# A four-layer graph network kernel: row products issued a stripe later, left terms spread earlier, and layer 2 in a fixed order

## The chip, the cores and the metric

The kernel runs on one core of one Trainium2 chip. The metric is the device time of one execution in microseconds (us), the median of several runs. In the text PE is TensorE (matrix products), DVE is VectorE, ACT is ScalarE, POOL is GpSimd, and SP is the queue that starts the large loads. SBUF is the working memory, and PSUM the memory into which PE writes[...].

## What is computed

x is 4096x64 and adj is a 4096x4096 matrix of zeros and ones, both float32. Four layers follow one another, each of the form x = layernorm(x + layer(x)). adj is read anew from main memory in each, 64 MiB a time. The reference, cut to what matters here:

```python
# layer 0: mean over the neighbours
h_neigh = (adj @ X + X) / deg;  out = relu(concat([X, h_neigh]) @ W + b);  out / norm(out)

# layers 1 and 3: attention in hyperbolic space, over all pairs (i, j)
left, right = x_t @ w_att[:D, 0], x_t @ w_att[D:, 0]
adj_att = sigmoid(left[:, None] + right[None, :] + b_att) * adj
x_local = logmap(x[:, None, :], x[None, :, :], c)
support_t = einsum('ij,ijd->id', adj_att, x_local);  proj(expmap(x, support_t, c), c)

# layer 2: weights that halve with the rank of a neighbour, counted from the end of the row
support = input @ weight                       # the "row products"
rank = cumsum(mask, axis=1);  k = min(deg, 100);  pos = rank - (deg - k)
w = mask * where(pos > 0, 0.5 ** (k - pos), 0);   out = w @ support + bias
```

## The kernel before

The 4096 receiving rows are cut into 4 **stripes** of 1024 (`GROUPS` = 3, 2, 1, 0), the sending rows into 32 **blocks** j of 128, taken from 31 down to 0. One **unit** is one stripe by one block: a tile of 128 x 1024 pairs. Each layer has 4 x 32 = 128 units. One load brings two blocks of one stripe (1 MiB).

The work on rows between the layers (normalisation, the curved step `move`, the row products `linear`, the preparation `prepare` of the next layer) is written as generators. They are queued with `later`, and `tick` takes a few steps of the queue after each unit, first come first served:

```python
def tick(n):
    while n and waiting:
        if next(waiting[0][1], False) is False: waiting.pop(0)
        else: n -= 1

def rsqrt(a, name):                              # 1/sqrt by bits and three Newton steps, on [P, 8]
    half = row.tile([P, n], I32, name="rs_half")
    V.tensor_scalar(half, a.bitcast(I32), 1, None, ALU.logical_shift_right)
    V.tensor_scalar(r.bitcast(I32), half, -1.0, float(0x5F3759DF), ALU.mult, ALU.add)
    for _ in range(3): ...                       # tensor_mul and two scalar_tensor_tensor each
```

Layers 1 and 3. `attend` is one stripe; DVE has two passes over each 128x1024 tile, ACT two, PE six products into `zp` and two (in float32, each issued as two) into `acc`:

```python
def attend(layer, s, left_b, sb, ps, rate):
    acc = ps.tile([P, W], F32, name="acc")
    for g in reversed(range(NB // 2)):
        _, edge = load(s, g)
        need((layer, 2 * g // WB))               # takes queue steps until this group's rows are there
        for k in (1, 0):
            zp = ps.tile([P, WW], F32, name="zp")            # two banks, 2 such tiles
            ...                                              # L861, L864, L867: products into zp
            nc.scalar.activation(sig, left_b, AF.Sigmoid, bias=right[:, j : j + 1])       # L869
            nc.scalar.activation(sq, zp, AF.Square, bias=turn, scale=-1.0 / UNIT)         # L873
            V.scalar_tensor_tensor(t, zp, 0.0, sig, ALU.max, ALU.mult)                    # L875
            V.scalar_tensor_tensor(t, sq, HIGH**2, t, ALU.add, ALU.mult)                  # L876
            ...                                              # L878: acc += xe[j] x t
            tick(rate)
    sums = sb.tile([P, W], F32, name="sums", bufs=1)
    nc.scalar.copy(sums, acc)                                # L884
    return sums

def attention(layer, x, x_new, curve, rates, behind):        # behind: linear (layer 1), store (layer 3)
    with ExitStack() as lp:                                  # pools of its own for each layer
        sb, ps = ...                                         # SBUF bufs=2; PSUM bufs=2
        need((layer, GROUPS[0])); left_b = spread_left(GROUPS[0])
        for n, s in enumerate(GROUPS):
            sums = attend(layer, s, left_b, sb, ps, rates[n])
            if n + 1 < NW: left_b = spread_left(GROUPS[n + 1])
            later((layer + 1, s), move(s, x, x_new, sums, curve, layer == 1), behind(s, x_new))
```

`spread_left` (8 transposes on PE, L837, two ACT copies, L842) puts the stripe's left terms on all partitions; every sigmoid of the stripe reads it. `move` turns a stripe's sums into its new rows: some 16 queue steps with three `rsqrt`, mostly a chain of DVE operations on [128, 8], from the transposes L891 to the sum x_new at L992. `linear` is 4 steps: transposes of the new rows (L1001), ACT copy (L1004), products with the weights (L1008), ACT (L1016) and DVE (L1017) into `halves`, which layer 2 multiplies by. `spread_left`, `move` and `linear` all take their PSUM tiles from `aux`, which has 2 buffers.

Layer 2 takes two stripes in turns. z holds running counts of neighbours in PSUM, w = 2^-z:

```python
with ExitStack() as lp:                          # pools of its own: d2_own, d2_sb (3), d2_ps (2)
    ...                                          # enter, pass_by: 0/1 matrices made here
    for n in range(0, NW, 2):
        two = GROUPS[n : n + 2]
        zs, accs = ..., ...                      # a z of two banks and an acc of one for each
        for g in reversed(range(NB // 2)):
            ...                                  # load and, for odd g, check(s, g, a) on DVE (L692)
            for k in (1, 0):
                for i, edge in enumerate(edges):
                    ...                          # L1209: 4 products into z (2 pass_by, 2 enter)
                    nc.scalar.activation(w, z, AF.Exp, bias=at_edge, scale=-LN2)          # L1217
                    ...                          # L1220: 4 products of w and halves[j] into acc
                    tick(1)
        for s, acc in zip(two, accs):
            nc.scalar.copy(sums, acc)            # L1230
            later((3, s), end_2(s, sums), prepare(s, x_3, ...))
```

The order of the instructions on each engine is otherwise not that of the text: the framework that compiles the kernel sorts them by a model of its own, within what data and buffers allow.

Of the kernel before, what the change touches and what calls it, by code (L numbers as in the profile page):

```python
# [10 lines left out]
F32 = mybir.dt.float32  # L11
# [10 lines left out]
D = 64  # L22
# [36 lines left out]
def gnn_stack_kernel(  # L59
# [511 lines left out]
    def stream(fits):  # L571

        with ExitStack() as st:
# [3 lines left out]

            keep = pool("f_keep")
            xs = pool("f_xs", 3)
            loads = pool("f_loads", 5)  # L580
            row = pool("f_row")
            lefts = pool("f_lefts", 2)
            aux = pool("f_aux", 2, space=PSUM)
# [44 lines left out]
            def rsqrt(a, name):  # L628

                n = a.shape[1]  # L630
                half = row.tile([P, n], I32, name="rs_half")
                V.tensor_scalar(half, a.bitcast(I32), 1, None, ALU.logical_shift_right)
                r, t = nums(name, n), nums("rs_t", n)
                V.tensor_scalar(
                    r.bitcast(I32), half, -1.0, float(0x5F3759DF), ALU.mult, ALU.add
                )
                for _ in range(3):
                    V.tensor_mul(t, r, r)
                    V.scalar_tensor_tensor(t, t, -0.5, a, ALU.mult, ALU.mult)
                    V.scalar_tensor_tensor(r, t, 1.5, r, ALU.add, ALU.mult)  # L640
                return r
# [200 lines left out]
                    nc.scalar.copy(to[:, h * W : (h + 1) * W], t)  # L842
                return to

            def attend(layer, s, left_b, sb, ps, rate):


                acc = ps.tile([P, W], F32, name="acc")
                for g in reversed(range(NB // 2)):
                    _, edge = load(s, g)  # L850
                    need((layer, 2 * g // WB))
                    for k in (1, 0):
                        j = 2 * g + k
                        of = slice(j * P, (j + 1) * P)

                        zp = ps.tile([P, WW], F32, name="zp")
                        for h in range(2):
                            half = zp[:, h * W : (h + 1) * W]
                            to = slice(s * WW + h * W, s * WW + (h + 1) * W)
                            at = k * WW + h * W  # L860
                            nc.tensor.matmul(  # L861
                                half, two_i, edge[:, at : at + W], start=True, stop=False
                            )
                            nc.tensor.matmul(  # L864
                                half, hi_lo[:, of], lo_hi[:, to], start=False, stop=False
                            )
                            nc.tensor.matmul(half, src[:, of], dst[:, to], start=False, stop=True)  # L867
                        sig = sb.tile([P, WW], F32, name="sig")
                        nc.scalar.activation(  # L869
                            sig, left_b, AF.Sigmoid, bias=right[:, j : j + 1]  # L870
                        )
                        sq = sb.tile([P, WW], F32, name="sq")
                        nc.scalar.activation(sq, zp, AF.Square, bias=turn, scale=-1.0 / UNIT)  # L873
                        t = sb.tile([P, WW], F32, name="t", bufs=3)
                        V.scalar_tensor_tensor(t, zp, 0.0, sig, ALU.max, ALU.mult)  # L875
                        V.scalar_tensor_tensor(t, sq, HIGH**2, t, ALU.add, ALU.mult)  # L876
                        for h in range(2):
                            nc.tensor.matmul(  # L878
                                acc[h * D : (h + 1) * D, :], xe[:, j, :], t[:, h * W : (h + 1) * W],
                                start=j == BLOCKS[0], stop=j == BLOCKS[-1],  # L880
                            )
                        tick(rate)
                sums = sb.tile([P, W], F32, name="sums", bufs=1)
                nc.scalar.copy(sums, acc)  # L884
                return sums

            def to_rows_of(sums):

# [130 lines left out]
                )  # L1019


            x0 = xs.tile([P, NB, D], F32, name="x")
            for s in GROUPS:
                nc.sync.dma_start(x0[:, blocks(s), :], x_in[:, blocks(s), :])
            x1 = xs.tile([P, NB, D], F32, name="x")
            with ExitStack() as lp:
# [47 lines left out]
                for s in GROUPS:  # L1074
# [49 lines left out]
                        prepare(s, x1, att1, batt1_sb, curve1, 1e-15, good[:, 0]),  # L1124
                    )

            def attention(layer, x, x_new, curve, rates, behind):
                with ExitStack() as lp:
                    sb = lp.enter_context(tc.tile_pool(name="n_sb", bufs=2))
                    ps = lp.enter_context(tc.tile_pool(name="n_ps", bufs=2, space=PSUM))  # L1130
                    need((layer, GROUPS[0]))
                    left_b = spread_left(GROUPS[0])
                    for n, s in enumerate(GROUPS):
                        sums = attend(layer, s, left_b, sb, ps, rates[n])
                        if n + 1 < NW:
                            left_b = spread_left(GROUPS[n + 1])
                        later(
                            (layer + 1, s), move(s, x, x_new, sums, curve, layer == 1),
                            behind(s, x_new),
                        )  # L1140


            x_2 = xs.tile([P, NB, D], F32, name="x")
# [3 lines left out]


            x_3 = xs.tile([P, NB, D], F32, name="x")
            with ExitStack() as lp:  # L1150
                own = lp.enter_context(tc.tile_pool(name="d2_own", bufs=1))
                sb = lp.enter_context(tc.tile_pool(name="d2_sb", bufs=3))
                ps = lp.enter_context(tc.tile_pool(name="d2_ps", bufs=2, space=PSUM))


                enter = own.tile([P, P], BF16, name="enter")
                pass_by = own.tile([P, P], BF16, name="pass_by")
                edge_of = own.tile([P, P], BF16, name="edge_of")
                V.tensor_scalar(edge_of, ident, OFF_EDGE, None, ALU.mult)
                V.memset(pass_by, 1.0)  # L1160
                nc.gpsimd.affine_select(
                    out=enter, in_=pass_by, compare_op=ALU.is_gt, fill=0.0, base=0,
                    pattern=[[-1, P]], channel_multiplier=1,
                )
                V.tensor_sub(enter, enter, edge_of)
                V.tensor_sub(pass_by, pass_by, enter)
                at_edge = num(own, "at_edge", 1)
                V.memset(at_edge, -(OFF_EDGE + CUT) * LN2)

                def end_2(s, sums):  # L1170
                    z = grp("z0")
                    t = to_rows_of(sums)
                    yield 1
                    V.scalar_tensor_tensor(
                        z.rearrange("p (h k) f -> p h k f", h=2)[:, 0], t[:, 0], 2.0**CUT / SUP,
                        b2_sb[:, None, :].to_broadcast([P, SB, D]), ALU.mult, ALU.add,
                    )
                    V.scalar_tensor_tensor(
                        z.rearrange("p (h k) f -> p h k f", h=2)[:, 1], t[:, 1], 2.0**CUT / SUP,
                        b2_sb[:, None, :].to_broadcast([P, SB, D]), ALU.mult, ALU.add,  # L1180
                    )
                    yield 1
                    V.tensor_add(z, z, x_2[:, blocks(s), :])
                    yield 1
                    yield from norm_rows(x_3, s, z, x2[:, blocks(s)])

                for n in range(0, NW, 2):
                    two = GROUPS[n : n + 2]
                    zs = [ps.tile([P, WW], F32, name="z") for _ in two]

                    accs = [ps.tile([P, W], F32, name="acc") for _ in two]
                    behind = [None, None]
                    for g in reversed(range(NB // 2)):
                        edges = []
# [6 lines left out]
                        for k in (1, 0):  # L1201
                            j = 2 * g + k
                            for i, edge in enumerate(edges):
                                z, acc = zs[i], accs[i]
                                here = edge[:, k * WW : (k + 1) * WW]
                                for lhs, rhs in ((pass_by, behind[i]), (enter, here)):
                                    for h in range(0, WW, W):
                                        if rhs is not None:
# [3 lines left out]
                                                skip_group_check=True,  # L1212
                                            )
                                behind[i] = here

                                w = sb.tile([P, WW], BF16, name="w")
                                nc.scalar.activation(w, z, AF.Exp, bias=at_edge, scale=-LN2)  # L1217
                                for part in range(2):
                                    for h in range(2):
                                        nc.tensor.matmul(  # L1220
                                            acc[h * D : (h + 1) * D, :],
                                            halves[:, j, part * D : (part + 1) * D],
                                            w[:, h * W : (h + 1) * W],
                                            start=j == BLOCKS[0] and part == 0,
                                            stop=j == BLOCKS[-1] and part == 1,
                                        )
                                tick(1)
                    for s, acc in zip(two, accs):
                        sums = row.tile([P, W], F32, name="sums2", bufs=2)
                        nc.scalar.copy(sums, acc)  # L1230
                        later(
                            (3, s), end_2(s, sums),
                            prepare(s, x_3, att3, batt3_sb, curve3, 1e-30, good[:, 1]),
# [96 lines left out]
```

## Time and profile before

| | |
|---|---|
| time, median of 3 runs | 1259.73 us (1249.18 to 1260.44) |
| the profiled execution | 1248.49 us, span 1246.8 us |
| busy PE, DVE, ACT | 1064.1, 981.3, 811.4 us of the span |
| layer 0 | 0 to about 216 us |
| layer 1, its four stripes' sums (L884) | 313, 396, 497, 604 us |
| layer 2, first and second pair of stripes | 619.5 to 734, and to 857 us |
| layer 3, then the last rows | 857 to 1219, and to 1246.8 us |

The stages are read from the first and last start of each line's instructions, and the copies of the sums. A table of stages gives, for each stretch, the us in which each engine was busy with the number of instructions in brackets, then the granted clock of PE as a share of full speed, the share of the DMA engines, and GB/s. A timeline row gives start, duration, engine, line, operation, count, and in square brackets how long the engine was idle before and which instruction released it. The busy time of PE counts overlapping products once, but the end of a product is modelled, so the distance between starts tells more than durations do.

### The profile page before, as it was taken

How to read it: one execution, taken by the hardware profiler on the slowest of the kernel's cores; microseconds unless marked ns; L12 is line 12 of the kernel's file. 1: busy time of each engine (PE TensorE's matmuls, PEld its weight loads, DVE VectorE, ACT ScalarE, POOL GpSimd, SP SyncE). 2: the span in 40 equal slices, each digit the busy share in tenths (PEclk: the TensorE clock that was granted, in tenths of full speed). 3: DMA queues.
4: the chain of work that ended last, by engine and by line, in shares of the span. 5: the costliest groups of instructions: out<-in, count | busy, mean ns of one | idle time of the engine just before them, and what ended most of it. 6: DMA issues, size and time to landing. Idle time of an engine off the chain costs nothing.

```text
span 1246.8 us, 13844 instructions
## 1 busy us (share of the span) xinstructions
PE 1064.1 (85%) x4818; PEld 393.4 (32%) x4907; DVE 981.3 (79%) x2081; ACT 811.4 (65%) x833; POOL 49.6 (4%) x85
## 2 busy tenths in 40 slices
PE   5879788899998899798598898898889999899990
PEld 2345445232222322322232223332333333222220
DVE  5486876999997799599663347535999999999996
ACT  0021213889886787587365668767889888788870
POOL 0010101000000000000100000000000000001001
PEclk9989899899999799699699999999999999999996
DMA  7989898555554366155177887688345555565510
GB/s 280 400 338 335 313 357 324 186 175 203 202 203 169 109 201 229 68 203 186 51 268 271 295 313 265 241 295 299 134 152 201 203 202 203 182 204 204 203 34 20
DMA packets 40144, 271.83 MB, mean 218 GB/s; under 512 B 6016, under 2 KB 6272, under 8 KB 7296
## 3 DMA queue, kind: packets, MB, share of 16 engines
q1 hardware_dynamic: 37440, 269.50, 61.0%
q10 hardware_dynamic: 2624, 1.35, 0.4%
q8 instruction: 40, 0.66, 0.2%
q14 instruction: 40, 0.33, 0.1%
HBM read 269.78 MB, written 1.05 MB: 217 GB/s over the span
## 4 chain that ended last, share of the span: by engine, by line
DVE 40%; PE 40%; ACT 12%; DMA 4%; issue 3%; POOL 1%; another core or an unknown queue 0%; ACTq 0%; POOLq 0%; SPq 0%; DVEq 0%
DVE t L875 14%; DVE t L876 13%; PE acc L878 7%; PE z L1209 6%; PE acc L1220 6%; ACT w L1217 5%; PE zp L861 4%; PE zp L864 4%; PE zp L867 4%; PE acc L1087 4%; ACT sq L873 3%; DVE junk L692 3%; DMA edges<-in_adj_dram 2%; PE aux L1008 2%; PE aux L775 1%
## 5 line engine op out<-in xcount | busy, mean ns | idle before, releaser
L873 ACT ACTIVATE sq<-zp,turn 128x1024 f32<-128x1024 f32 x256 | 285.1, 1114 | 84.1 <-PE zp L867 52.9
L875 DVE SCALAR_TENSOR_TENSOR t<-zp,sig 128x1024 f32<-128x1024 f32 x256 | 311.3, 1219 | 15.3 <-ACT sq L873 12.9
L876 DVE SCALAR_TENSOR_TENSOR t<-sq,t 128x1024 f32<-128x1024 f32 x256 | 311.0, 1220 | 0.8
L869 ACT ACTIVATE sig<-left_b,right 128x1024 f32<-128x1024 f32 x256 | 292.1, 1143 | 19.9 <-DVE t L875 18.0
L878 PE MATMUL acc<-t,xe 128*64 128x512 f32 x1024 | 282.2, 624 | 16.6 <-DVE t L876 15.9
L692 DVE SCALAR_TENSOR_TENSOR junk<-edges 128x2048 bf16<-128x2048 f32 x64 | 146.4, 2288 | 94.2 <-DMA edges<-in_adj_dram 94.2
L861 PE MATMUL zp<-edges,two_i 128*128 128x512 bf16 x461 | 181.3, 393 | 37.8 <-DVE t L875 34.1
L864 PE MATMUL zp<-lo_hi,hi_lo 128*128 128x512 f16 x512 | 195.5, 382 | 3.7 <-issue 0.4
L867 PE MATMUL zp<-dst,src 74*128 74x512 f16 x512 | 196.7, 384 | 0.0
L1217 ACT ACTIVATE w<-z,at_edge 128x1024 bf16<-128x1024 f32 x128 | 136.1, 1113 | 76.3 <-PE z L1209 74.0
L861 PEld LDWEIGHTS <-two_i 128*128 128x128 bf16 x512 | 50.2, 98 | 178.9 <-issue 141.7
L1220 PE MATMUL acc<-w,halves 128*64 128x512 bf16 x512 | 80.9, 393 | 25.0 <-ACT w L1217 24.5
L1087 PE MATMUL acc<-edges,first 128*128 128x512 bf16 x240 | 79.0, 406 | 16.7 <-DMA edges<-in_adj_dram 16.3
L878 PEld LDWEIGHTS acc<-t,xe 128*64 128x64 f32 x1024 | 51.8, 136 | 124.5 <-DVE t L876 64.6
L1209 PE MATMUL z<-edges,enter 128*128 128x512 bf16 x245 | 85.4, 393 | 2.2 <-DVE k L909 1.6
L1087 PE MATMUL acc<-edges,third 128*65 128x512 bf16 x256 | 83.2, 407 | 0.8 <-issue 0.2
L867 PEld LDWEIGHTS <-src 74*128 74x128 f16 x512 | 49.4, 96 | 101.0 <-issue 42.2
L864 PEld LDWEIGHTS <-hi_lo 128*128 128x128 f16 x512 | 50.1, 98 | 86.0 <-issue 50.3
L1209 PE MATMUL z<-edges,pass_by 128*128 128x512 bf16 x237 | 75.0, 394 | 1.7 <-issue 1.5
L1220 PEld LDWEIGHTS <-halves 128*64 128x64 f16 x512 | 24.1, 108 | 75.6 <-issue 74.6
L1107 ACT COPY top<-acc 128x512 f32<-128x512 f32 x8 | 4.7, 588 | 63.7 <-PE acc L1087 63.7
L1209 PEld LDWEIGHTS <-enter 128*128 128x128 bf16 x256 | 24.2, 97 | 52.3 <-issue 28.9
(255 smaller groups left out, 784.4 us busy)
## 6 DMA issues: line engine op xcount, KB each, us to landing
edges<-in_adj_dram SPq DMA_DIRECT2D x256, 1024.0 KB, 5.0
x<-in_x_dram SPq DMA_DIRECT2D x4, 256.0 KB, 3.9
out_dram<-x ACTq DMA_DIRECT2D x4, 256.0 KB, 2.5
att_sb<-in_L_gnn_w_att_dram ACTq DMA_DIRECT2D x1, 64.0 KB, 7.3
att_sb<-in_L_gnn_att_w_dram ACTq DMA_DIRECT2D x1, 64.0 KB, 6.1
w_sb<-in_L_gnn_W_dram ACTq DMA_DIRECT2D x1, 32.0 KB, 3.7
b_sb<-in_L_gnn_b_dram ACTq DMA_DIRECT2D x1, 32.0 KB, 4.1
b_sb<-in_L_gnn_bias_dram ACTq DMA_DIRECT2D x1, 32.0 KB, 5.2
```

The lines of the kernel that those rows point to most:

```text
L692: V.scalar_tensor_tensor(junk, a, 0.0, a, ALU.not_equal, ALU.not_equal, accum_out=odd[:, n : n + 1])
L861: nc.tensor.matmul(half, two_i, edge[:, at : at + W], start=True, stop=False)
L864: nc.tensor.matmul(half, hi_lo[:, of], lo_hi[:, to], start=False, stop=False)
L867: nc.tensor.matmul(half, src[:, of], dst[:, to], start=False, stop=True)
L869: nc.scalar.activation(sig, left_b, AF.Sigmoid, bias=right[:, j : j + 1])
L873: nc.scalar.activation(sq, zp, AF.Square, bias=turn, scale=-1.0 / UNIT)
L875: V.scalar_tensor_tensor(t, zp, 0.0, sig, ALU.max, ALU.mult)
L876: V.scalar_tensor_tensor(t, sq, HIGH**2, t, ALU.add, ALU.mult)
L878: nc.tensor.matmul(acc[h * D : (h + 1) * D, :], xe[:, j, :], t[:, h * W : (h + 1) * W], start=j == BLOCKS[0], stop=j == BLOCKS[-1],)
L1087: nc.tensor.matmul(accs[h][:m], lhs[:, j, :], edge[:, at : at + W], start=j == BLOCKS[0], stop=j == BLOCKS[-1],)
L1209: nc.tensor.matmul(z[:, h : h + W], lhs, rhs[:, h : h + W], start=j == BLOCKS[0], stop=True, skip_group_check=True,)
L1217: nc.scalar.activation(w, z, AF.Exp, bias=at_edge, scale=-LN2)
```

## The change

It does five things. (1) Row products: `behind` (in layer 1, `linear`) is no longer queued with its stripe's `move`, but after the next stripe's `attend`, ahead of that stripe's `move`. (2) Left terms: `spread_left` for the next stripe is issued at the load g = 2 of the running one, six units ahead of its end. (3) Layer 2 has a fixed order on PE and ACT, that of the text; in it, the products L1220 of a unit are put off (`lag`) until after the next unit's products into z. (4) Pools: attention and layer 2 share one SBUF and one PSUM pool, opened once; w takes the place of `sq`; the 0/1 matrices are made at the start of the kernel; and the loads have 6 buffers in place of 5. (5) `rsqrt` makes its first guess with one DVE operation in place of two.

The diff, cut to its core (left out are the moved lines that make the 0/1 matrices, and `end_2`, which is moved unchanged):

```diff
-            loads = pool("f_loads", 5)
+            loads = pool("f_loads", 6)
@@ rsqrt
-                half = row.tile([P, n], I32, name="rs_half")
-                V.tensor_scalar(half, a.bitcast(I32), 1, None, ALU.logical_shift_right)
                 V.tensor_scalar(
-                    r.bitcast(I32), half, -1.0, float(0x5F3759DF), ALU.mult, ALU.add
+                    r.bitcast(I32), a.bitcast(I32), -0.5, float(0x5F3759DF), ALU.mult, ALU.add
                 )
@@ attend
-            def attend(layer, s, left_b, sb, ps, rate):
+            def attend(layer, s, left_b, rate, then):
+                next_left = None
                     need((layer, 2 * g // WB))
+                    if g == 2 and then is not None:
+                        next_left = spread_left(then)
-                        zp = ps.tile([P, WW], F32, name="zp")
+                        zp = ps.tile([P, WW], F32, name="z")
-                sums = sb.tile([P, W], F32, name="sums", bufs=1)
+                sums = row.tile([P, W], F32, name="sums", bufs=2)
-                return sums
+                return sums, next_left
@@ attention
+            sb = pool("p_sb", 2)
+            ps = pool("p_ps", 2, space=PSUM)
             def attention(layer, x, x_new, curve, rates, behind):
-                    for n, s in enumerate(GROUPS):
-                        sums = attend(layer, s, left_b, sb, ps, rates[n])
-                        if n + 1 < NW:
-                            left_b = spread_left(GROUPS[n + 1])
-                        later(
-                            (layer + 1, s), move(s, x, x_new, sums, curve, layer == 1),
-                            behind(s, x_new),
-                        )
+                behind_of = None
+                for n, s in enumerate(GROUPS):
+                    then = GROUPS[n + 1] if n + 1 < NW else None
+                    sums, left_b = attend(layer, s, left_b, rates[n], then)
+                    if behind_of is not None:
+                        later((layer + 1, behind_of), behind(behind_of, x_new))
+                    later((layer + 1, s, "x"), move(s, x, x_new, sums, curve, layer == 1))
+                    behind_of = s
+                later((layer + 1, behind_of), behind(behind_of, x_new))
@@ layer 2
+            lag = []
+            def flush():
+                while lag:
+                    lag.pop(0)()
+            with tc.manual_schedule(engines={mybir.EngineType.PE, mybir.EngineType.Activation}):
                 for n in range(0, NW, 2):
...
                                 behind[i] = here
+                                flush()
-                                w = sb.tile([P, WW], BF16, name="w")
+                                w = sb.tile([P, WW], F32, name="sq").bitcast(BF16)[:, :WW]
                                 nc.scalar.activation(w, z, AF.Exp, bias=at_edge, scale=-LN2)
-                                for part in range(2):
-                                    for h in range(2):
-                                        nc.tensor.matmul(acc[...], halves[...], w[...], ...)
+                                def add(acc=acc, j=j, w=w):
+                                    ...          # the same four products
+                                lag.append(add)
                                 tick(1)
+                    flush()
```

## The prediction

> **What bounds the kernel now.** I read the table of stages first, because the share of busy time of the whole span (PE 85%, DVE 79%) mixes stages with different limits. I cut the span where a line starts or ends: at the copies of the stripes' sums and at the first work after them.
>
> ```profile
> core 0: us, PE busy (x) PEld busy (x) DVE busy (x) ACT busy (x) POOL busy (x), PEclk, DMA share, GB/s
> 313.00:396.00 83.00, 80.10 (x322) 24.46 (x324) 81.70 (x140) 69.89 (x67) 1.28 (x1) 1.00 0.60 204
> 396.00:413.00 17.00, 8.63 (x38) 6.80 (x37) 5.99 (x17) 6.98 (x12) 2.21 (x2) 0.64 0.14 56
> 413.00:497.00 84.00, 81.08 (x314) 24.53 (x319) 80.78 (x141) 68.10 (x64) 0.63 (x1) 0.97 0.57 192
> 497.00:514.00 17.00, 8.95 (x38) 6.97 (x37) 5.62 (x14) 7.05 (x12) 2.38 (x2) 0.58 0.10 41
> 514.00:602.00 88.00, 78.21 (x298) 23.47 (x303) 84.11 (x141) 66.44 (x61) 0.46 (x1) 0.96 0.52 179
> 602.00:619.50 17.50, 9.81 (x34) 6.06 (x36) 7.98 (x25) 4.39 (x8) 2.05 (x3) 0.50 0.00 1
> 619.50:734.00 114.50, 102.51 (x516) 33.89 (x524) 48.79 (x115) 69.69 (x70) 2.63 (x2) 0.99 0.77 272
> 734.00:857.00 123.00, 107.97 (x603) 38.47 (x613) 60.27 (x173) 90.55 (x97) 4.26 (x14) 0.99 0.79 280
> ```
>
> Within a stripe of layer 1 (313 to 396, 413 to 497) DVE is busy 81.7 of 83 and 80.8 of 84 us: DVE is the bound there. The groups say why:
>
> ```profile
> L875 DVE SCALAR_TENSOR_TENSOR t<-zp,sig 128x1024 f32<-128x1024 f32 x256 | 311.3, 1219 | 15.3 <-ACT sq L873 12.9
> L876 DVE SCALAR_TENSOR_TENSOR t<-sq,t 128x1024 f32<-128x1024 f32 x256 | 311.0, 1220 | 0.8
> ```
>
> Two passes of 1.22 us for 128 units are 312 us a layer; nothing in the change touches them. Layer 3 has the same loop, so layers 1 and 3 can lose only idle DVE time, and that lies between stripes: from 396 to 413 and from 497 to 514 DVE works 6.0 and 5.6 of 17 us, and from 602 to 619.5 it works 8.0. The boundaries of layer 3 show no such hole. The chain of waits names what fills the first one:
>
> ```profile
> 397.75 1.57 POOL w_att L988
> ...
> 405.06 1.97 PE aux L1008 x8
> 407.03 2.05 PE aux L837 x8
> ```
>
> `move` of the stripe before ends (L988, L992), then its row products run one engine after another (L1001, L1004, L1008 from 400.1 to 407.0), and only then the left terms of the next stripe (L837), without which no sigmoid can start; the next z on PE (L861) comes at 413.4. So 17 us are a queue for the two `aux` buffers: the left terms depend on none of this and merely come later in the text. Why does a `move` whose first transpose (L891) is at 314 end only at 399? The timeline of DVE:
>
> ```profile
> 389.63 0.22 DVE L973 TENSOR_SCALAR n<-n,k_rsc 128x8 f32<-128x8 f32 x1
> 389.76 1.22 DVE L876 SCALAR_TENSOR_TENSOR t<-sq,t 128x1024 f32<-128x1024 f32 x1
> ...
> 390.90 0.16 DVE L974 TENSOR_SCALAR n<-n 128x8 f32<-128x8 f32 x1
> 390.97 1.22 DVE L876 SCALAR_TENSOR_TENSOR t<-sq,t 128x1024 f32<-128x1024 f32 x1
> ```
>
> Its chain of short operations gets one turn between two long passes: some 65 dependent steps of 1.25 us are a whole stripe of 82 us.
>
> Layer 2 is another regime. ACT and PE, in turns, there:
>
> ```profile
> 672.08 2.12 ACT L1217 ACTIVATE w<-z,at_edge 128x1024 bf16<-128x1024 f32 x2 [1.43 <-PE z L1209]
> 675.63 2.12 ACT L1217 ACTIVATE w<-z,at_edge 128x1024 bf16<-128x1024 f32 x2 [1.43 <-PE z L1209]
> ```
>
> ```profile
> 673.24 0.62 PE L1220 MATMUL acc<-w,halves 128*64 128x512 bf16 x4 [0.36 <-ACT w L1217]
> 673.80 0.62 PE L1209 MATMUL z<-edges,pass_by 128*128 128x512 bf16 x2
> ```
>
> A pair of units takes 3.55 us (672.08 to 675.63). ACT does two exps in 2.12 us and then waits 1.43 us for z. PE waits too, 0.36 us for w, at the head of each such cycle. Neither is full: both exps run together, and PE then has products for both. The largest work is PE's. From starts, two products 0.22 to 0.23 us apart (a row of two lasts 0.61, a single one 0.39), so 4 into z are 0.90 us; the 4 into acc, which lie in two halves of the array, 0.56 us (673.24 to 673.80). A unit is 1.46 us of PE against 1.06 of ACT.
>
> **What the Trainium skill says.** "PSUM — Partial Sum Buffer", section "Engine vs sequencer instructions": products start and complete in the order of the program, and the queues of ScalarE and VectorE are strict first in, first out. The trace agrees: L837 sits behind L1008 although its data are older. It also means that a fixed order holds every exp behind whatever row work stands in front of it. "Perfetto Trace Analysis", section "Optimization Strategy": with several regimes one treats each by itself and looks for what blocks in the gaps of its engine; a gap that repeats can mean that there are too few buffers. Layer 2 has such a gap, but here the order on PE makes it, for both z exist. "TensorE: Matmul & The Clock Gate", section "HAM oscillation — how this bites in real kernels": PE that idles falls to half its clock. The table agrees, 0.64, 0.58 and 0.50 in the three gaps; so the first products after a gap are slow as well.
>
> **The change part by part.**
>
> *Row products and left terms, layer 1.* Both 17 us gaps should close, as `linear` now follows a `move` that had a whole stripe, and the left terms are there before the stripe ends. The 11.6 us of DVE work in the gaps do not vanish: they go into stripes where DVE is full. I allow 1.5 us a boundary for the sums and refilling, as in layer 3 (DVE idle of 1.3 to 2.8 us a stripe by the table). Gain: 34 − 11.6 − 3 = **19 us**.
>
> *Into layer 2.* The third `move` now starts later, behind a `linear`, so it isn't done when layer 1 ends. When its stripe is over, the remaining steps have DVE to themselves, 0.2 us each. In the fixed order PE's first row work in layer 2 is the `linear` of that stripe; it holds PE until x_new is there. I estimate 8 us of the 17.5 remain (15 to 20 steps at 0.2 us, POOL's 1.57, DVE's 0.69, the first exp's table). Layer 2 has idle DVE time, so the rest is gained: **9 us**. The shared pools are needed for this, as nothing waits for a pool to be given back.
>
> *Layer 2.* In the new order, PE does z(u+1) between z(u) and the acc products of u. From the end of z(u), 0.1 us to the exp (the last product ends at 675.53, the exp starts at 675.63), 1.11 of exp, 0.05 to PE (673.19 to 673.24) are 1.26 us; PE has acc(u−1) and z(u+1) to do meanwhile, 1.46 us. So PE needn't wait: a pair is 2.92 us, and 64 pairs take 187 against 227 us. DMA: a pair needs 1 MiB, 361 GB/s; layer 0 reached 409 in a stretch of 25 us (50 to 75), and the sixth buffer gives room. On PE then comes the row work that was hidden in the slack: two `linear` (3.4 us each: twice 0.6 and 1.1, from layer 0's rows), two `prepare` (four sets of transposes at 0.91, and 0.34), sums to rows, together 18 us. Last, stalls of the fixed order: a Square, a cast, a tanh or a transpose stands in the queue when DVE has yet to compute its input, perhaps behind a 2.28 us `check`. Some five such places for each of two prepared stripes and three for the `move`, each 0.5 to 2 us: 12 us by estimate. The sum is 217 us against 237.5: **20 us**.
>
> *Small ones.* One operation less in each `rsqrt`: about 28 of them lie in DVE-bound stretches, 0.1 us each in between long passes, and three in the last rows: **3 us**. Left terms ahead of time in layer 3: **3 us**. The sixth buffer in layer 0, where DMA moves 334 GB/s over the layer but 409 in its best stretch: the short stops at the stripes' ends may close a little, **3 us**.
>
> Together 57 us.
>
> **The rivals.** *(a) The fixed order eats its own gain.* ACT in layer 2 has 0.40 us of slack a unit; the copies of `prepare` take 1.01 each, and only one unit is held back in `lag`. Against it: the text leaves whole steps between a DVE operation and its reader in several places, and only some 80 of 128 units have a step. If stalls were 30 us instead of 12, layer 2 would gain nothing, and the kernel would be at 1215. *(b) A gap moves instead of closing.* `move` plus a late `linear` may spill over each stripe, some 10 us more each time, and be paid before layer 2: PE would stand 15 us or more. For it: a `move` fills its stripe already. The time would be about 1206. *(c) DMA becomes the bound in layer 2.* At 2.92 us a pair the tiles held by `behind` and `check` leave few loads in flight; at layer 0's mean of 334 GB/s a pair takes 3.14 us, and 14 us of the gain go. *(d) All better:* with stalls near nothing, and the table's full 17.5 us gained, 1175.
>
> **Range and chances.** The profiled span is 1246.8, the median 12 above it, the lowest run 2. From the middle of the measured times, 1254, less 57: 1196 us, with its uncertainty mostly in layer 2 (0 to 35 us) and at its entry (0 to 15). Range 1168 to 1224. Faster by over 2% means below 1234.5, which needs only half of layer 1's and a part of layer 2's gain: 0.91. Within 2%: 0.07. Slower: 0.02, if the order of the whole program shifts for the worse.
>
> **What would show it.** In the profile after: stripes of layer 1 end some 84 us apart with no stretch where DVE is under 8 tenths, and L837 before each L884; first exp within 10 us of the last L884 of layer 1; ACT's waits for z (74 us by the waits of now) falling to a third, exps 1.46 us apart in the stretches without row work, and PE's clock at full there; layer 2's first exp to last L1230 near 217 us. The prediction is wrong if exps stay 1.7 us apart or more because PE waits for loads or ACT stands behind row work, or if DVE in layer 1 idles at other places.

## The result, and the profile after

| | before | after |
|---|---|---|
| time, median | 1255.7 us (4 runs) | 1209.26 us (4 runs, 1208.16 to 1209.93) |
| ratio, 95% interval | | 0.9633 (0.9579 to 0.9687) |
| span of the profiled execution | 1246.8 us | 1206.4 us |

The prediction was 1196 us, range 1168 to 1224. The chain of stages, cut at the copies of the stripes' sums (L884 and L1230 before, L886 and L1248 after), shows where the 40.3 us of span came from:

| stage | before | after | difference |
|---|---|---|---|
| layer 0 and first stripe of layer 1 | 313.8 | 311.7 | −2.1 |
| second stripe | 82.5 | 82.3 | −0.1 |
| third stripe | 100.9 | 89.6 | −11.3 |
| fourth stripe | 107.0 | 95.7 | −11.3 |
| layer 2, from the sums of layer 1 to its own last sums | 252.5 | 234.9 | −17.6 |
| layer 3 | 362.0 | 364.1 | +2.1 |
| last rows | 28.2 | 28.1 | 0.0 |

Differences are taken before rounding. The medians differ by 46.4 us: the profiled execution of before took 7 us less than its median, that of after 1 us less, so 6 us of the gain are in no stage of this table.

The table of stages of the changed kernel, in the columns of the one shown for before:

```profile
394.00:411.00 17.00, 15.23 (x59) 4.68 (x59) 16.30 (x25) 13.72 (x14) 1.97 (x1) 1.00 0.60 218
...
484.00:500.00 16.00, 15.74 (x65) 4.90 (x63) 15.68 (x28) 14.32 (x14) 0.00 (x0) 1.00 0.60 219
...
579.50:590.40 10.90, 1.99 (x8) 1.01 (x10) 7.25 (x28) 1.00 (x3) 1.21 (x1) 0.50 0.00 1
590.40:697.00 106.60, 103.98 (x550) 33.72 (x550) 46.58 (x114) 74.49 (x74) 2.84 (x2) 0.99 0.81 290
697.00:814.50 117.50, 109.06 (x610) 35.40 (x610) 61.20 (x169) 88.77 (x93) 9.34 (x14) 0.97 0.80 291
```

Where the first hole of layer 1 was, DVE is busy 16.3 of 17 us, and 15.7 of 16 where the second was. A hole is left ahead of layer 2 (579.5 to 590.4), with PE at half clock. The exps in layer 2, by groups: they wait for z 52 us instead of 74, where I had forecast a third of 74.

```profile
L1228 ACT ACTIVATE sq<-z,at_edge 128x1024 bf16<-128x1024 f32 x128 | 142.1, 1113 | 52.6 <-PE z L1219 52.3
```

The timeline of an undisturbed stretch, ACT and then PE. Each row is one exp, or the products of half a unit:

```profile
641.15 1.11 ACT L1228 ACTIVATE sq<-z,at_edge 128x1024 bf16<-128x1024 f32 x1 [0.45 <-PE z L1219]
642.71 1.11 ACT L1228 ACTIVATE sq<-z,at_edge 128x1024 bf16<-128x1024 f32 x1 [0.45 <-PE z L1219]
```

```profile
642.54 0.62 PE L1235 MATMUL acc<-sq,halves 128*64 128x512 bf16 x4
643.09 0.62 PE L1219 MATMUL z<-edges,pass_by 128*128 128x512 bf16 x2
643.56 0.61 PE L1219 MATMUL z<-edges,enter 128*128 128x512 bf16 x2
644.10 0.62 PE L1235 MATMUL acc<-sq,halves 128*64 128x512 bf16 x4
644.65 0.62 PE L1219 MATMUL z<-edges,pass_by 128*128 128x512 bf16 x2
```

The exps are 1.56 us apart, against 1.78 (half of a pair of 3.55) before, and PE has no bracket, so it doesn't wait. But 1.56 is not the 1.46 of the prediction. From start to start, the two pass_by products take 0.47 us, the two enter products ahead of acc 0.54, and the four acc products 0.55. Two products inside z take 0.45 elsewhere (see x8).

The entry of layer 2, PE:

```profile
588.41 1.03 PE L1003 MATMUL aux<-ident,x 128*64 128x128 f32 x4 [9.13 <-DVE x L994]
```

The fixed order has the transposes of the third stripe's new rows here (L1003), and they wait for the last step of that stripe's `move` (L994).

### The profile page after: what moved, and what is told of

Same layout as the page of the kernel before. It is cut to its first block, busy times and chain, and to the rows that moved or that the text cites. A ratio compares the mean times of both kernels' runs of the same rounds, so it can differ in the third digit from the quotient of the medians.

```text
span 1206.4 us, 13877 instructions
## 1 busy us (share of the span) xinstructions
PE 1063.5 (88%) x4907; PEld 381.6 (32%) x4907; DVE 975.7 (81%) x2035; ACT 812.8 (67%) x831; POOL 56.2 (5%) x85
## 4 chain that ended last, share of the span: by engine, by line
PE 46%; DVE 40%; ACT 6%; DMA 4%; issue 3%; POOL 1%; ACTq 0%; POOLq 0%; DVEq 0%; SPq 0%
DVE t L877 13%; DVE t L878 11%; PE acc L880 9%; PE z L1219 8%; PE z L863 6%; PE z L869 5%; PE z L866 5%; PE acc L1235 4%; PE acc L1106 4%; DVE junk L690 4%; ACT sq L875 3%; DMA edges<-in_adj_dram 2%; PE aux L773 2%; PE aux L1010 1%; ACT sq L1228 1%
## 5 line engine op out<-in xcount | busy, mean ns | idle before, releaser
L875 ACT ACTIVATE sq<-z,turn 128x1024 f32<-128x1024 f32 x256 | 285.0, 1113 | 78.7 <-PE z L869 52.8
L877 DVE SCALAR_TENSOR_TENSOR t<-z,sig 128x1024 f32<-128x1024 f32 x256 | 311.4, 1219 | 15.0 <-ACT sq L875 11.9
L880 PE MATMUL acc<-t,xe 128*64 128x512 f32 x1024 | 289.1, 625 | 15.9 <-DVE t L878 15.6
L863 PE MATMUL z<-edges,two_i 128*128 128x512 bf16 x512 | 201.6, 394 | 28.2 <-DVE t L877 24.1
L869 PE MATMUL z<-dst,src 74*128 74x512 f16 x512 | 196.5, 384 | 0.0
L866 PE MATMUL z<-lo_hi,hi_lo 128*128 128x512 f16 x512 | 195.3, 381 | 0.0
L1228 ACT ACTIVATE sq<-z,at_edge 128x1024 bf16<-128x1024 f32 x128 | 142.1, 1113 | 52.6 <-PE z L1219 52.3
L1106 PE MATMUL acc<-edges,first 128*128 128x512 bf16 x256 | 82.5, 402 | 17.5 <-DMA edges<-in_adj_dram 17.2
L1235 PE MATMUL acc<-sq,halves 128*64 128x512 bf16 x512 | 81.2, 397 | 9.1 <-ACT sq L1228 9.1
L869 PEld LDWEIGHTS <-src 74*128 74x128 f16 x512 | 49.4, 96 | 98.5 <-issue 40.3
L1219 PE MATMUL z<-edges,enter 128*128 128x512 bf16 x256 | 79.9, 394 | 0.0
L773 PE MATMUL aux<-ident,ys 128*128 128x128 f16 (+1 forms) x192 | 19.1, 268 | 28.7 <-DVE ys L754 28.7
```

What stands on the lines that cost most here:

```text
L863: nc.tensor.matmul(half, two_i, edge[:, at : at + W], start=True, stop=False)
L866: nc.tensor.matmul(half, hi_lo[:, of], lo_hi[:, to], start=False, stop=False)
L880: nc.tensor.matmul(acc[h * D : (h + 1) * D, :], xe[:, j, :], t[:, h * W : (h + 1) * W], start=j == BLOCKS[0], stop=j == BLOCKS[-1],)
L1106: nc.tensor.matmul(accs[h][:m], lhs[:, j, :], edge[:, at : at + W], start=j == BLOCKS[0], stop=j == BLOCKS[-1],)
L1219: nc.tensor.matmul(z[:, h : h + W], lhs, rhs[:, h : h + W], start=j == BLOCKS[0], stop=True, skip_group_check=True,)
```

## The experiments

In each set the kernel before ran on the same chip, and its median moves by up to 8 us from set to set; so ratios are compared first. A profile gives the lengths of stages.

| run | median us | ratio to before (95%) |
|---|---|---|
| the change | 1209.3 | 0.9633 (0.9579 to 0.9687) |
| x1 parts (1) and (2) alone | 1230.9 | 0.985 (0.9803 to 0.9897) |
| x3 no fixed order | 1204.6 | 0.9644 (0.9588 to 0.97) |
| x4 no late acc products | 1386.4 | 1.109 (1.1014 to 1.1166) |
| x5 row products at once | 1232.3 | 0.9876 (0.9848 to 0.9903) |
| x6 left terms at the end | 1207.8 | 0.9669 (0.9646 to 0.9692) |
| x7 empty steps ahead of row products | 1191.1 | 0.9543 (0.9519 to 0.9566) |
| x8 acc products in pairs | 1199.8 | 0.9602 (0.9578 to 0.9626) |
| x9 five load buffers | 1215.8 | 0.9732 (0.9685 to 0.9779) |
| x10 left terms a stripe early, row products at once | 1217.3 | 0.9744 (0.9703 to 0.9785) |
| x11 = x7 and x8 | 1181.0 | 0.9445 (0.9421 to 0.9468) |
| x12 = x8, no fixed order | 1196.0 | 0.9573 (0.9547 to 0.96) |
| x13 = x11, DVE and ACT spaced | 1179.7 | 0.9442 (0.9412 to 0.9471) |

### x1: only the row products and left terms

```diff
  # the kernel before, with parts (1) and (2) of the change as in its diff;
  # pools, layer 2, loads and rsqrt stay
```

> The kernel before with only parts (1) and (2): row products a stripe later, left terms at g = 2; pools, layer 2, loads and rsqrt as before. My theory: the two gaps of layer 1 close by these two alone, 22 to 23 us (the stripes' ends of the changed kernel came 11.3 us earlier each), so about 1233 us; layer 2 from its first exp on stays at 237 us. Rival: the gaps close only with the shared pools or the new rsqrt; then this run is within 5 us of before, 1255.

The third and fourth stripes end after 88.4 and 89.8 us: both gaps close with these two parts alone. They are 30 us shorter than before (100.9 + 107.0 less 88.4 + 89.8). The fourth is even shorter than the changed kernel's 95.7, in part because only 1.6 us of layer 2's checks (L692) run in it, against 6.3 there. But 9 us are given back at once: from the start of the last sums of layer 1 to the first exp it is now 24.2 us, against 15.3. The table of stages for nearly that stretch:

```profile
577.70:601.30 23.60, 7.83 (x30) 5.77 (x32) 13.50 (x49) 3.80 (x6) 2.04 (x3) 0.50 0.00 1
```

PE first waits 13.2 us for the third stripe's new rows (L995); then the late row products of that stripe come due, serially, with nothing of layer 2 beside them. So (1) moves part of its cost to the entry of layer 2.

### x5, x6, x10: which of the two closes the gaps

x5 undoes part (1), x6 part (2); x10 is x5 with the left terms a whole stripe early:

```diff
  # x5 and x10
-                    if behind_of is not None:
-                        later((layer + 1, behind_of), behind(behind_of, x_new))
-                    later((layer + 1, s, "x"), move(...))
-                    behind_of = s
-                later((layer + 1, behind_of), behind(behind_of, x_new))
+                    later((layer + 1, s), move(...), behind(s, x_new))
  # x10 besides
-                    if g == 2 and then is not None:
+                    if g == (2 if s == GROUPS[0] else NB // 2 - 1) and then is not None:
  # x6
-                    if g == 2 and then is not None:
-                        next_left = spread_left(then)
+                    # spread_left(then) after the stripe's sums, as before
```

> The changed kernel with part (1) undone: the row products are queued right behind their stripe's move again, the left terms stay ahead (part 2). My theory (the gaps were the left terms queueing behind the row products for the aux buffers): the left terms alone close the gaps, stripes 3 and 4 of layer 1 end within 3 us of the changed kernel's 89.6 and 95.7 us, total within 5 us of 1209. Rival: the row products themselves hold PE at the stripe's start, 8 us a boundary or more stay, 1225 or more.

> The changed kernel with part (2) undone: left terms spread after the stripe's end, row products still a stripe late. My theory: with the row products out of the way the aux buffers are free, the left terms take the 2 us they take in layer 3 of the kernel before, so some 2 to 3 us a boundary and six boundaries, but part of it hidden: 1212 to 1222 us. Rival: the left terms still wait for move's own aux use or the late row products; gaps of 10 us or more come back, 1230 or more.

> The changed kernel with part (1) undone, as in x5, but the left terms of the third and fourth stripe spread at the start of the stripe before (g = 15), so that they stand ahead of the row products in the text too. In x5 the left terms (L835) still ran straight behind the row products (L1010): at g = 2 they come later in the text than row products queued some 20 units into the stripe. My theory (a queue for the two aux buffers in the order of the text): now the left terms are there early, the sigmoids of the next stripe start at once, and the gaps of 17 us fall under 6: stripes of 89 to 95 us as in the changed kernel, total near 1215. Rival: PE, in order, is held by the row products themselves until x_new is there, whatever the left terms do: gaps of 10 us or more stay, stripes near 100 us, total near 1232 as in x5.

x5 went against me: stripes of 100.9 and 101.8 us, the gaps are back. Its chain of waits shows why:

```profile
391.17 1.57 POOL w_att L990
...
398.25 1.97 PE aux L1010 x8
400.22 2.05 PE aux L835 x8
```

L835, the left terms, still comes straight after the row products. Those are queued some 17 to 20 units into the stripe, and g = 2 is the 27th unit: in the text the left terms are still the later ones, behind row products whose rows aren't there yet. x10 puts the left terms first in the text and leaves the row products where they were; the stripes fall to 91.8 and 93.2 us. The table of stages of x10, at the two boundaries:

```profile
394.00:411.00 17.00, 15.47 (x62) 4.82 (x60) 16.66 (x24) 13.65 (x14) 1.97 (x1) 1.00 0.63 220
486.00:502.00 16.00, 15.81 (x64) 4.96 (x63) 15.57 (x25) 14.22 (x14) 0.00 (x0) 1.00 0.68 239
```

DVE is full through both. So the place of the left terms behind the row products made the gaps, as the prediction said. That `aux` is what ties the two, and not the order on PE, is argued rather than shown. For the row products did not stay where they were in time: with DVE full, the new rows of x10 come at 410 us instead of 393 in x5, their transposes (L1003) follow only then, and PE has no wait for them in layer 1. A run with an `aux` buffer more, which could part the two, was not made. What ends the gaps is either order in which left terms don't stand behind row products that lack their rows.

x6 shows that (2) by itself is worth nothing here: stripes of 89.6 and 94.9 us, as in the changed kernel. Two rows of each timeline, of x6 and then of the changed kernel, show the third stripe's left terms:

```profile
321.39 0.58 ACT L840 COPY left_b<-aux 128x512 f32<-128x512 f32 x1
...
324.96 0.58 ACT L840 COPY left_b<-aux 128x512 f32<-128x512 f32 x1
```

```profile
317.73 0.58 ACT L840 COPY left_b<-aux 128x512 f32<-128x512 f32 x1
...
321.30 0.58 ACT L840 COPY left_b<-aux 128x512 f32<-128x512 f32 x1
```

The second stripe had started at 315.4 in x6 and at 311.7 in the changed kernel. The third stripe starts at 397.7 and 394.1, so with the row products out of the way the framework itself issues the left terms some 70 us ahead of need, wherever of these two places the text has them. x10 pays elsewhere (19.5 us from the last sums to the second exp), so its total is 1% above the change's.

### x3, x4: fixed order or late products

```diff
  # x3
-            with tc.manual_schedule(engines={mybir.EngineType.PE, mybir.EngineType.Activation}):
+            if True:
  # x4
                                 lag.append(add)
+                                flush()
```

> The changed kernel without the fixed order on PE and ACT in layer 2; acc products still put off by a unit in the text. My theory: the put-off text alone isn't kept, the framework sorts the exps into pairs again, so units go back towards 1.75 us and the run is some 15 us slower than the changed kernel, 1225. Rival: the late products are enough, and the fixed order only costs stalls behind row work (26 us in layer 2 and 9 us at its entry); then this run is 10 to 20 us faster, about 1195.

> The changed kernel with the fixed order, but each unit's acc products straight after its exp. My theory: PE then waits for every exp, 1.26 us from the end of z to w, so a unit takes 1.56 + 1.26 = 2.8 us and layer 2 some 160 us more: about 1370 us. Rival: PE has other work or the exp overlaps, and the run stays within 20 us of the changed kernel.

x4 tests the late products alone, for its fixed order leaves the framework no choice. PE's timeline there:

```profile
700.91 0.62 PE L1235 MATMUL acc<-sq,halves 128*64 128x512 bf16 x4 [1.26 <-ACT sq L1228]
...
703.81 0.62 PE L1235 MATMUL acc<-sq,halves 128*64 128x512 bf16 x4 [1.26 <-ACT sq L1228]
```

PE waits 1.26 us in each undisturbed unit, the very sum of 0.1, 1.11 and 0.05 that the prediction made from the rows of before. A unit is 2.89 us, and the kernel is 11% slower than the one before.

x3 has no fixed order, and its units take the same 1.56 us in undisturbed stretches; PE's timeline:

```profile
661.32 0.62 PE L1235 MATMUL acc<-sq,halves 128*64 128x512 bf16 x4
661.87 0.62 PE L1219 MATMUL z<-edges,pass_by 128*128 128x512 bf16 x2
662.34 0.61 PE L1219 MATMUL z<-edges,enter 128*128 128x512 bf16 x2
662.88 0.62 PE L1235 MATMUL acc<-sq,halves 128*64 128x512 bf16 x4
```

z and acc alternate just as in the changed kernel, from acc to acc 1.56 us (661.32 to 662.88). So the pairs of exps were not what the framework insists on: with the late products in the text it keeps to them, and my theory of x3 was wrong. Before and x1, whose units come in pairs, lack the late products but also the shared pools; shared pools without either late products or fixed order were not tried, so what ends the pairs in x3 is in part argued. The fixed order has a price and a return: without it PE is busy 12.3 of the 12.5 us after the last sums of layer 1, while the changed kernel's PE waits 9.1 us at this place; the first pair of stripes takes 107 us to its last sums instead of 118, but the second takes 123.5 instead of 117, and layer 3's first stripe 3 us more. In total the two can't be told apart.

x1 also has no fixed order, yet its first exp comes 24.2 us after the last sums of layer 1, while x3 has exps before them and after them without a stop. x3 differs from it in pools, late acc products, load buffers and `rsqrt`. The shared pools are the likely cause, for with them layer 2 need not wait until the pool of layer 1 is given back; alone they were not tried.

### x7: the price of the fixed order at the entry

```diff
+                    if layer == 1 and then is None:
+                        later("pause", pause(8))         # eight queue steps that do nothing
                     if behind_of is not None:
                         later((layer + 1, behind_of), behind(behind_of, x_new))
 ...
+                if layer == 1:
+                    later("pause", pause(4))
                 later((layer + 1, behind_of), behind(behind_of, x_new))
```

> The changed kernel with 8 empty queue steps ahead of the third stripe's row products and 4 ahead of the last one's, so that the fixed order of layer 2 meets them later. My theory: PE's 9.1 us wait at the entry of layer 2 (for x_new of the third stripe) and the 1.9 us wait at 624 are the price of the fixed order; both go, 9 to 12 us faster than the changed kernel: about 1198. Rival: DVE only finishes that move later because something else is then in its way, and the wait comes back at another place: within 3 us of 1209.

From the last sums of layer 1 to those of layer 2's first pair it is 104.2 us, against 118.2; the second pair and layer 3 are within 1.2 us of the change's. (The 4 us by which this profile is shorter up to the first sums of layer 1 lie ahead of the edit.) The ratio falls by 0.009, some 11 us, with intervals apart. Nothing else took the wait's place: DVE has idle time there, so it ends the `move` while PE has units to do: PE has no wait for L998, the line of x_new here, in layer 2.

### x8: the missing 0.10 us

```diff
-                                flush()
+                                if i == 1:
+                                    flush(1)             # both stripes' acc products, after both z
-                                w = sb.tile([P, WW], F32, name="sq")...
+                                w = sb.tile([P, WW], F32, name=("sq", "sig")[k])...
```

> The changed kernel, with the acc products of both stripes' units put off together: PE does z, z, acc, acc in place of z, acc, z, acc (w takes four buffers of sq and sig). A unit in the changed kernel is 1.56 us, 0.10 more than my sum of 0.90 and 0.56; in its rows the step from the last z product to the first acc product is 0.54 where others are 0.45. My theory: that step is the cost of going from full-width to half-width weights; halved in number, a unit is 1.51 and layer 2 some 6 us shorter: 1203. Rival: PE is held by exp or by loads at 1.56, or the step comes with every z group: no gain, or slower since two exps then run together.

PE's timeline, one pair of units:

```profile
655.85 0.62 PE L1219 MATMUL z<-edges,pass_by 128*128 128x512 bf16 x2
656.31 0.61 PE L1219 MATMUL z<-edges,enter 128*128 128x512 bf16 x2
656.76 0.61 PE L1219 MATMUL z<-edges,pass_by 128*128 128x512 bf16 x2
657.22 0.61 PE L1219 MATMUL z<-edges,enter 128*128 128x512 bf16 x2
657.76 1.05 PE L1236 MATMUL acc<-sq,halves 128*64 128x512 bf16 x8
658.75 0.62 PE L1219 MATMUL z<-edges,pass_by 128*128 128x512 bf16 x2
```

The step from enter to acc is still 0.54, but there is one for two units. A pair is 2.90 us (655.85 to 658.75), a unit 1.45. The saving is 0.11 us a unit where I expected 0.05, and the rows say why: eight acc products now take 0.99 (657.76 to 658.75), two times 0.50, where four took 0.55. So the way back from acc to z costs about 0.1 as well, and both changes of kind are paid half as often. That 1.45 is the 1.46 of the prediction is chance: its 0.56 for acc held one change, and it lacked the other. Of the 14 us that 0.11 in 128 units would make, the trace shows half: layer 2's stretch is 228 us against 235, and the fourth stripe ahead of it is 2 us longer. Where the rest went was not found; the profiled execution was the slowest of its four. The times show little (0.9602 against 0.9633, intervals overlapping), so only the pace of a unit is shown, not a gain of the whole kernel.

### x9: the sixth load buffer

```diff
-            loads = pool("f_loads", 6)
+            loads = pool("f_loads", 5)
```

> The changed kernel with 5 load buffers. My theory: loads bind only in layer 0 (2 us gained there by the sixth buffer), layer 2 at 290 GB/s has room: 1211 to 1213 us. Rival: at the faster pace of layer 2 five buffers are too few, DMA becomes its bound: 1220 us or more, with PE waiting for edges.

Between the two: 5.2 us of span, 2.0 up to the first sums of layer 1 and 3.6 in layer 2. There PE's two waits for new rows (L994) are 6.6 and 4.0 us in place of 9.1 and 1.9, in sum nearly the same, so they don't explain the 3.6. The waits list none of PE for edges in layer 2, so PE isn't bound by DMA with five buffers; `check` on DVE, though, waits 59.5 us for them from 590 to 820 us, against 48.8, so loads may well come later. By times it is 1% slower than the change, with intervals that just touch.

### x11, x12, x13: together

```diff
  # x11: the edits of x7 and x8.  x12: x8 with "if True:" as in x3.
  # x13: x11, and in norm_rows and prepare
                 V.tensor_sub(v, v, over(m))
+                yield 1
                 nc.scalar.activation(sq, v, AF.Square)
  # and likewise ahead of the cast of y and of the two logarithms
```

> x7's empty steps and x8's paired acc products together. If the two savings are independent (entry of layer 2: 18 us of total in x7; unit of 1.45 in place of 1.56 us: 5 to 9 us in x8), 1184 us. Rival: with the entry gone, PE meets row work and loads at the same moments, and only one of the two counts: 1191.

> x8 without the fixed order. x3 showed that the late products alone give 1.56 us a unit with no fixed order. Theory now: the fixed order isn't what made layer 2 faster; the framework keeps z, z, acc, acc too, enters layer 2 without the wait for x_new, and loses some in the second pair: 1193 to 1200. Rival: without the fixed order it interleaves z and acc products, the switch costs come back, and the run is at 1204 as x3.

> x11 with one queue step more between a DVE operation and its ACT reader at three places (Square in norm_rows, the casts and the logarithms in prepare). Theory: the stalls of the fixed order in the second pair of layer 2 are ACT standing before data of DVE (3.5 us for the casts of the first prepared stripe, 9 us of PE waiting for w in all); spaced, 4 to 6 us go: 1179. Rival: PE is full there with row work (109 of 119 us busy in x7) and the spacing only moves it: within 2 us of x11.

x11 is 5.6% faster than before and beats the change by 0.019 in the ratio, intervals far apart: the two savings add up, if not more (0.009 and 0.003 in the ratio by themselves). Its PE is busy 95.45 of 95.6 us in layer 2's first pair:

```profile
578.00:673.60 95.60, 95.45 (x549) 38.81 (x549) 51.59 (x139) 69.57 (x74) 4.05 (x3) 1.00 0.89 332
673.60:789.20 115.60, 107.03 (x617) 42.08 (x616) 60.98 (x169) 89.90 (x96) 7.17 (x14) 0.94 0.81 299
```

Without the fixed order, x12 keeps pairs of acc products in the first pair of stripes, 99 us against 107 in x3, but mostly breaks them up in the second, 123 against 123.5. So the rival was right in part. The rest of its lead on x3 is layer 3's first stripe (105.6 against 114), which the edit doesn't touch. It is 1.3% behind x11, whose pairs of stripes take 95.5 and 115.5 us. The two differ by the empty steps as well as the fixed order, but x12 has no wait at the entry that empty steps could take away; so a fixed order whose entry is mended seems to be worth its price. x13 shortens x11's second pair of stripes to 108.6, yet its time is that of x11; layer 0 happened to be 3 us longer in its profile. Whether the spacing is worth its 7 us is open.

## Why the prediction was right, point by point

- *Layer 1, 19 us:* 22.6 measured, by the cause given. But of the two parts that the prediction names, the row products' place in the queue does it; the left terms at g = 2 do nothing (x5, x6). A whole stripe early they close the gaps alone (x10).
- *Entry, 9 us gained, 8 left:* 4 gained, 11 left. One exp now runs ahead of the last sums; from these to the second exp it is 11.1 us, where it was 15.3 to the first; the wait for x_new in the fixed order is the one described (9.13 us), and x7 removes it.
- *Layer 2, 20 us:* 13.3 measured from the first regular exps on (223.8 us from 590.4 to the end, 237.1 before). The term that was mis-sized is the unit: 1.46 us by adding 0.90 and 0.56, 1.56 in fact, 13 us over 128 units. The sum took the two halves from rows of before; the 0.56 for acc held the change back to z, but the 0.90 for z, from steps inside z, lacked the change to acc. It stood in that trace too: a single product of z started at 674.26 and the first of acc at 674.58, 0.32 us, where single steps inside z are 0.22 to 0.24. The other two terms hold: 30 us were allowed for row work and stalls, and 224 less 127 units of 1.56 leaves 26.
- *"PE needn't wait":* right, and x4 gives the 1.26 us. That it takes the fixed order: not so (x3).
- *Rival (a)*, stalls eat the gain: mainly at the entry; in the second pair of stripes there are some too, for x13 is 7 us shorter there. *Rival (b)*, a gap that moves: partly true, in x1 outright (9 us), in the change as the wait for x_new. *Rival (c)*, DMA: no; layer 2 moves 277 GB/s on average, and PE has no wait for edges there.
- *Small ones, 9 us:* in sum nothing. Layer 0 and the first stripe gave 2; layer 3 lost 2. Its later stripes are 1.5, 0.2 and 1.4 us shorter, in sum the 3 us that the prediction gave to early left terms. But these are not the cause: the three stripes take 253.3 us, and 252.4 in x6, which has no early left terms, but 257.2 in x1, which has them (256.4 before). So the gain lies with the other parts, likely (4) or (5); neither was run alone, but for the sixth load buffer (x9). The first stripe of layer 3 is 110.8 instead of 105.6. DVE does the same work in it but is idle for 11.1 us against 5.6, in stops of 0.4 to 2.6 us; why there are more of them was not found, and in the other runs the stripe takes from 105.6 to 114.
- *The sum:* 57 against 40 in the profile. The 17 us that it was too high are 9 here, 7 in layer 2 and 5 at its entry, less 4 that layer 1 gave more.
- *The signs:* two of them could not come by the prediction's own figures. The third and fourth stripes were to be 84 us long, but 207.9 us less the 19 forecast is 94 each (89.6 and 95.7 measured). ACT's waits for z were to fall to a third of 74, but 0.40 us of slack in 128 units is 51 (52 measured). In its sums, 1 MiB in 2.92 us is 359 GB/s and not 361, and 1254 less 57 is 1197.

## What to carry to other kernels

Work whose inputs come late can hold back other work that stands behind it in the text, here probably through a buffer pool that both use. So put late work late, or early work first, and check in the chain that the order has really changed. When two engines wait for each other in turns and neither is full, put the consumer off by one unit; a fixed order is a separate matter, and has a price wherever a fixed instruction lacks its data. To predict the new pace of a full engine, measure the steps between kinds of work as well as the work.

## What the runs showed of the hardware

From the start of the last two z products (over 128 columns of weights) to that of the first acc product (over 64 columns) it took 0.54 us, where two steps among z products took 0.45 to 0.47: some 0.09 us more. The way back costs about as much: four products into acc followed by z took 0.55, eight 0.99. Both are paid once a unit or once a pair by order alone (1.56 and 1.45 us a unit). The two kinds of products differ in their operands and their place in PSUM as well as in width; which of these costs the time was not separated.
